# A hybrid of two state-space mixers and two feed-forward parts: the order of the steps behind a chunk's output projection

## The chip, the cores and the metric

The kernel runs on one core of one Trainium2 chip. The metric is the device time of one execution in microseconds (us); the figures of before are the median of three runs, and one further execution was taken by the hardware profiler.

## The reference, cut to what matters

The input is x of 4 sequences, 1024 tokens and 512 features, in float32. Four parts follow one another, each on the layer norm of what stands and added to it: mixer A, a feed-forward part, mixer B, the same feed-forward part again. Both mixers are state-space layers of 1024 inner channels. A has 16 heads of 64 channels and a state of 64, B has 64 heads of 16 channels and a state of 128. What the change touches is this much of a mixer:

```python
gate, hBC, dt = split(x @ in_proj)            # B: the same with factors on the parts
hBC = silu(causal_conv4(hBC) + conv_b)        # h, B, C
dt = softplus(dt + dt_bias)
# per head, over the tokens: state = state * exp(dt * A) + (dt * h) B^T ;  y = C state + D h
yf = y * silu(gate)                           # B: norm first, then the gate
var = mean(yf * yf)                           # over the 1024 channels
out = (norm_w * yf * rsqrt(var + eps)) @ out_proj
```

The kernel works in chunks of 128 tokens: what a chunk's tokens give each other comes from a 128 x 128 matrix of decays for every head, and what earlier chunks give comes from the state carried between chunks.

## The kernel before

**Tiles and stages.** A chunk is 128 tokens, a group is two chunks, and a mixer has 16 groups, so 32 chunks, four groups to a sequence. Two generators are woven together for each group: `chunk`, which runs the state-space part of the present group's two chunks, and `front`, which projects, convolves and gates the group after it. `front` also carries `norm`, the layer norm of the group after that. All four compute engines take their instructions in the order in which Python issues them; only the DMA queue on SyncE is ordered by the scheduler. What waits at the head of an engine's list holds all that stands behind it.

**The weave.** Each `yield` of `chunk` adds an amount to `due`, and steps of `front` are issued until their amounts have used it up. When `front` has nothing left the inner loop ends. Single small matmuls stand in the list `small`: one is issued behind each large matmul of `front` (line 347), and `finish` issues what is left of a part. `later_on` holds instructions for other engines that are issued one step later.

**front.** 18 steps: 8 half gates (product `pz`, line 347; tanh on ScalarE, line 536; `z` on VectorE, line 541) and 9 or 10 convolution tiles (product `pc`, line 347; first tap on ScalarE, line 470; three taps on VectorE, line 474). The small products `pd` for dt (line 503) go between those of gates 0 and 1, and line 511 adds the bias to each on VectorE as soon as it is issued. `softplus` starts at step 6 (lines 548 and 549) and goes on through lines 555 to 601.

**chunk.** In this order, the two mixers alike at the start:

- `fold`, two additions on VectorE that bring the chunk before's squares down to 256 columns (lines 971 and 972);
- `decays(0)`, four products `seg` in four PSUM banks (lines 789 and 799), with exponentials on ScalarE (line 806);
- the first step of the chunk before's `tail`;
- `from_state`: the two products `po` with the state (line 847), weighed on VectorE into `yo` (line 851);
- `hdr` and the state's decay on GpSimd (lines 919 and 928);
- the weighing of the decays on VectorE (line 813), the inner products `py` (lines 860 and 829), the sums into `h` (line 878), the squares (line 881 or 885), the gating on GpSimd (line 882), the state's update (`pst`, lines 898 to 909).

Mixer B goes through `decays` four times (0 to 3), mixer A once.

**tail.** In its first step it issues the 8 matmul pairs of the output projection `pout` (line 670) with the 4 short ones of the squares' sum `ssq` (line 672) between the last of them, and leaves the copy of `pout` (line 679), the scaling of `ssq` (line 680) and the power -1/2 on GpSimd (line 223) for `later_on`. In its second step the factor is finished and x updated (lines 685 and 686), the result stored (line 687, on ScalarE's queue) and its statistics taken (lines 229 to 232). Before, the first step stands behind `decays(0)` and the second behind `decays(1)` in B, and behind the weighing in A.

**prologue.** Thirteen small steps that prepare a chunk: five into the bank `misc` (lines 734 to 750) and eight transposes `tph` of h (line 709), weighed on VectorE into `hdt` (line 713); line 727 scales h by D on ScalarE.

**PSUM.** All products but `py` share one pool `mm` of seven banks; `py` has one bank. A tile of the pool takes a bank when it is first asked for, and its first matmul waits for the last reader of the tile that stood there before.

Of the kernel before, what the change touches and what calls it, by code (L numbers as in the profile page):

```python
# [21 lines left out]
KE = E // P  # L22
# [50 lines left out]
def hybrid_kernel(  # L73
# [37 lines left out]
    nc = tc.nc  # L111
# [38 lines left out]
    ones = const.tile([P, P], F32, tag="ones", name="ones")  # L150
# [96 lines left out]
    def mixer(m, in_w, conv_w, conv_b, dt_bias, A_log, Dv, norm_w, out_w, src, dst, first, stats, last_steps={}):  # L247
# [18 lines left out]
        with stack:  # L266
# [176 lines left out]
            def front(f, behind):  # L443
# [51 lines left out]


                v = sm.tile([P, GC, NH], F32, tag="v", name=f"v_{tag}", bufs=1)
                pds = []

                def project_dt(c, k):  # L500
                    if k == 0:
                        pds.append(mm(f"pd_{tag}_{c}"))
                    nc.tensor.matmul(
                        pds[c][:, :NH],
                        xnT[:, k, HIST + c * P : HIST + (c + 1) * P],
                        w_in[:, k, m.dt0 : m.dt0 + NH],
                        start=(k == 0),
                        stop=(k == KD - 1),
                    )
                    if k == KD - 1:  # L510
                        nc.vector.tensor_add(v[:, c, :], pds[c][:, :NH], dtb)

                defer(v, [lambda c=c, k=k: project_dt(c, k) for c in range(GC) for k in range(KD)], True)

# [29 lines left out]
                def softplus():  # L544

                    finish(v)
                    dt = f.dt = sm.tile([P, GC, NH], F32, tag="dt", name=f"dt_{tag}")
                    nc.vector.tensor_scalar_max(dt, v, 0.0)
                    nc.vector.scalar_tensor_tensor(v, dt, -2.0, v, ALU.mult, ALU.add)
                    yield  # L550
                    exu = wk.tile([P, 512], F32, tag="t2k", name=f"exu_{tag}", bufs=4)
                    ex, u1 = (
                        exu[:, i * GC * NH : (i + 1) * GC * NH].rearrange("p (c h) -> p c h", c=GC) for i in (0, 1)
                    )
                    nc.scalar.activation(ex, v, AF.Exp)
                    yield

                    nc.vector.tensor_scalar_add(u1, ex, 2.0)
                    nc.vector.reciprocal(u1, u1)
                    nc.vector.tensor_mul(ex, ex, u1)  # L560
                    nc.vector.tensor_mul(u1, ex, ex)
                    nc.vector.tensor_scalar_mul(v, u1, LOG_TERMS[0])
                    yield
                    for term in LOG_TERMS[1:-1]:
                        nc.vector.scalar_tensor_tensor(v, v, term, u1, ALU.add, ALU.mult)
                    nc.vector.scalar_tensor_tensor(v, v, LOG_TERMS[-1], ex, ALU.add, ALU.mult)
                    nc.vector.tensor_add(dt, dt, v)
                    yield
                    a = f.a = sm.tile([P, GC, NH], F32, tag="a", name=f"a_{tag}")
                    nc.vector.tensor_mul(a, dt, Ab.unsqueeze(1).to_broadcast([P, GC, NH]))  # L570
                    nc.vector.tensor_scalar(a, a, A_MIN * A_SCALE, 1.0 / A_SCALE, ALU.max, ALU.mult)

                    parts = wk.tile([P, 512], F32, tag="t2k", name=f"parts_{tag}", bufs=4)
                    parts = parts[:, : GC * 2 * HP].rearrange("p (c i h) -> p c i h", c=GC, i=2)
                    if HP > NH:
                        nc.gpsimd.memset(parts, 0.0)
                    hi, lo = parts[:, :, 0, :NH], parts[:, :, 1, :NH]
                    nc.vector.tensor_scalar(hi, a, A_ROUND, A_ROUND, ALU.add, ALU.subtract)
                    nc.vector.tensor_sub(lo, a, hi)
                    yield  # L580
                    yield
                    pcs = mm(f"pcs_{tag}")
                    for c in range(GC):
                        nc.tensor.matmul(
                            pcs[: 2 * HP, c * P : (c + 1) * P],
                            parts[:, c, :, :].rearrange("p i h -> p (i h)"),
                            le,
                            start=True,
                            stop=True,
                        )  # L590

                    rows = slice(0, 2 * HP)
                    ncs = wk.tile([P, 512], F32, tag="t2k", name=f"ncs_{tag}", bufs=4)
                    two = wk.tile([P, 2, GT], F16, tag="two", name=f"two_{tag}")
                    nc.scalar.activation(ncs[rows, :GT], pcs[rows, :GT], AF.Identity, scale=sign[rows])
                    nc.scalar.activation(two[rows, 0], pcs[rows, :GT], AF.Identity, scale=sign[rows])
                    nc.vector.tensor_sub(two[rows, 1], ncs[rows, :GT], two[rows, 0])
                    f.cs = dram.tile([GC, 2 * HP // 4, 2, 4, P], F16, tag="cs", name=f"csd_{tag}")
                    for c in range(GC):
                        for j in range(2):  # L600
                            nc.sync.dma_start(f.cs[c, :, j], two[rows, j, c * P : (c + 1) * P])
                    yield
# [56 lines left out]
            def tail(f, c, sqs):  # L659

                i = f.b * NCH + f.g * GC + c
                tag = f"{m.name}_{i}"
                cols = slice(c * P, (c + 1) * P)


                pout = mm(f"pout_{tag}")
                ssq = mm(f"ssq_{tag}")
                for e in range(KE):
                    on = dict(start=(e == 0), stop=(e == KE - 1))
                    nc.tensor.matmul(pout, f.hs[e // 2][:, e % 2, cols], w_out[:, e, :], **on)  # L670
                    if e >= KE - 2:
                        nc.tensor.matmul(
                            ssq[:, 0:1], sqs[0][:, e - KE + 2, :], ones[:, 0:1], start=(e == KE - 2), stop=(e == KE - 1)
                        )
                po = wk.tile([P, D], F32, tag="t2k", name=f"out_{tag}", bufs=4)
                rs = sm.tile([P, 1], F32, tag="rs", name=f"rs_{tag}", bufs=1)

                def leave():
                    nc.scalar.copy(po, pout)  # L679
                    nc.vector.tensor_scalar(rs, ssq[:, 0:1], 1.0 / E, m.eps, ALU.mult, ALU.add)  # L680
                    rsqrt(rs)

                later_on.append(leave)
                yield
                nc.vector.tensor_scalar_mul(rs, rs, gc)  # L685
                nc.vector.scalar_tensor_tensor(f.xs[c], po, rs, f.xs[c], ALU.mult, ALU.add)
                later_on.append(lambda: nc.scalar.dma_start(dst[i], f.xs[c]))

                layer_stats(sm, f.xs[c], 1e-5, "g", f"g{tag}", out=stats[:, i, 0:2])
                later_on.append(  # L690
                    lambda: nc.vector.scalar_tensor_tensor(
                        stats[:, i, 2:3], stats[:, i, 0:1], -1.0, stats[:, i, 1:2], ALU.mult, ALU.mult
                    )
                )
                yield
# [67 lines left out]
            def chunk(f, c, following):  # L763
# [147 lines left out]

                state.pop("fold", lambda: None)()
                L0 = decays(0)
                next(last, None)
                if not begin:
                    from_state()
                if not end:
                    hdr = wk.tile([P, E], F32, tag="hdr", name=f"hdr_{tag}")
                    nc.gpsimd.tensor_mul(
                        hdr.rearrange("p (n u d) -> p n u d", u=HC, d=HD),  # L920
                        packed(hdt, slice(0, NH // HC)),
                        er.rearrange("p (n u) -> p n u", u=HC).unsqueeze(3).to_broadcast([P, NH // HC, HC, HD]),
                    )
                    if begin:
                        Sp = wk.tile([P, SW], F32, tag="S", name=f"S_{tag}")
                    else:
                        Sp = state["S"]
                        nc.gpsimd.tensor_mul(heads_of(Sp), heads_of(Sp), over_head(et, P, NH // SH))
                yield 2.0
                weigh(L0)  # L930
                if CG == 4:
# [4 lines left out]
                    py, on = open_y(0)  # L936
                    for half in range(2):
                        inner(0, L0, half, py, on)
                    L2 = decays(2)
                    yield 3.0  # L940
                    weigh(L2)
# [15 lines left out]
                else:  # L957
                    next(last, None)
                    yield 2.5
                    to_state()  # L960
                    yield 2.0
                    for half in range(2):
                        py, on = open_y(half)
# [17 lines left out]
            with tc.manual_schedule(  # L981
# [23 lines left out]
                for n in range(len(groups)):  # L1005
# [5 lines left out]
                    for c in range(GC):  # L1011
                        following = (f, c + 1) if c + 1 < GC else (None if ahead is None else (ahead, 0))
                        for us in chunk(f, c, following):
                            due += us
                            while due > 0.0:
                                waiting, later_on[:] = later_on[:], []
                                piece = next(pieces, None)
                                for step in waiting:
                                    step()
                                if piece is None:  # L1020
                                    break
                                due -= piece
                            catch_up()
# [443 lines left out]
```

## Time and profile before

| | |
|---|---|
| median of 3 runs | 3053.41 us (3053.19 to 3053.58) |
| the profiled execution | 3044.65 us, of which its span 3042.9 us |
| granted TensorE clock, mean | 0.963 |
| busy: TensorE, VectorE, ScalarE, GpSimd | 91%, 68%, 41%, 24% |

By stage, from the view of windows:

| stage, us of the span | TensorE busy | VectorE busy | granted clock |
|---|---|---|---|
| first group of A, 0 to 94 | 71.55 | 54.24 | 0.91 |
| mixer A, 94 to 1160 | 1012.67 | 706.09 | 0.98 |
| feed-forward and the start of B, 1160 to 1427 | 247.84 | 154.77 | 0.97 |
| mixer B, 1427 to 2815 | 1255.13 | 1032.13 | 0.96 |
| feed-forward, 2815 to 3043 | 180.75 | 134.44 | 0.94 |

PE is TensorE's matmuls, PEld its weight loads, DVE is VectorE, ACT ScalarE, POOL GpSimd, SP SyncE. A line of a timeline gives the start in the span, the duration, engine, source line, operation, out<-in, shapes, a count, and in brackets how long the engine had been idle and what ended that. In the view of waits a line gives who waited for whom, then the total in us, the number of times and the longest. Names of tiles are shown without their numbers.

### The profile page before, as it was taken

To read this page: it belongs to the slowest core of one execution; us is meant where nothing else is said; L and a number is where in the kernel's file an instruction comes from. 1 tells how busy PE (TensorE), PEld (TensorE's weight loads), DVE (VectorE), ACT (ScalarE), POOL (GpSimd) and SP (SyncE) were. 2 spreads that over 40 slices of the span, in tenths; PEclk is the share of its full clock that TensorE was granted. 3 is DMA by queue.
4 is the path that set the end of the run, shared out by engine and by line. 5 is a ranking of instruction groups with operands and counts; after the bars stand their busy time and mean duration, and the time that the engine had idled before them with its cause. 6 is when DMAs were issued, how large, how long until landed. Compare 5 with 4: busy or idle time off the path is not lost. (4 is left out here: it accounts for less than half of the span.)

```text
span 3042.9 us, 46127 instructions
## 1 busy us (share of the span) xinstructions
PE 2767.9 (91%) x17156; PEld 1789.5 (59%) x17156; DVE 2081.7 (68%) x4417; ACT 1261.8 (41%) x2874; POOL 720.3 (24%) x839
## 2 busy tenths in 40 slices
PE   7999999999999988999999899999888888898986
PEld 5666666666666653456666666666555565564332
DVE  5667666766666662477777687776787777875368
ACT  3334433334333332355444444444444444443245
POOL 1222122122212221351111112212222222212057
PEclk8999999999999999999999999999999999998999
DMA  3000000000000015430000000000000000001423
GB/s 117 14 19 16 16 16 17 24 17 17 16 17 22 10 68 205 154 102 10 17 20 20 13 20 18 13 17 21 22 25 21 20 23 20 13 11 72 170 88 110
DMA packets 92959, 124.25 MB, mean 41 GB/s; under 512 B 38728, under 2 KB 42328, under 8 KB 92736
## 3 DMA queue, kind: packets, MB, share of 16 engines
q1 hardware_dynamic: 80960, 98.23, 10.0%
q10 hardware_dynamic: 9792, 16.82, 1.5%
q0 software_dynamic: 1984, 6.26, 0.6%
q8 instruction: 136, 2.23, 0.3%
q14 instruction: 87, 0.71, 0.1%
HBM read 84.54 MB, written 36.72 MB: 40 GB/s over the span
## 5 line engine op out<-in xcount | busy, mean ns | idle before, releaser
L347 PE MATMUL pc_b<-xnT_b,w_in_b 128*128 128x259 f32 x1280 | 355.7, 408 | 25.1 <-DVE S_b L909 21.9
L813 DVE TENSOR_TENSOR L_b<-L_b,Gm_b 128x1024 f32<-128x1024 f32 x256 | 308.7, 1247 | 2.9 <-ACT L_b L806 2.9
L347 PE MATMUL pz_a<-xnT_a,w_in_a 128*128 128x256 f32 x1024 | 296.5, 408 | 2.9 <-ACT Bt_a L756 2.3
L347 PE MATMUL pc_a<-xnT_a,w_in_a 128*128 128x259 f32 x1152 | 299.1, 394 | 0.0
L806 ACT ACTIVATE L_b<-seg_b 128x512 f32<-128x512 f32 x512 | 263.6, 603 | 74.0 <-PE seg_b L799 74.0
L347 PE MATMUL pz_b<-xnT_b,w_in_b 128*128 128x256 f32 x1024 | 291.4, 397 | 2.9 <-ACT xnT_b L436 2.9
L474 DVE SCALAR_TENSOR_TENSOR u_b<-pc_b,cw_b,u_b 128x256 f32<-128x256 f32 x480 | 231.5, 482 | 79.8 <-ACT u_b L470 68.3
L347 PEld LDWEIGHTS pc_b<-xnT_b,w_in_b 128*128 128x128 f32 x1280 | 229.3, 198 | 92.7 <-DVE S_b L909 25.4
L474 DVE SCALAR_TENSOR_TENSOR u_a<-pc_a,cw_a,u_a 128x256 f32<-128x256 f32 x432 | 208.2, 482 | 73.6 <-ACT u_a L470 63.3
L1205 PE MATMUL g_ps<-gw,xnT_f 128*128 128x512 f32 x512 | 246.9, 619 | 9.6 <-DMA gw<-in_L_ffn_gate_w 4.2
L829 PE MATMUL py_b<-L_b,hdt_b 128*32 128x128 f32 x4096 | 165.7, 299 | 97.6 <-DVE L_b L813 96.5
L670 PE MATMUL pout_a<-w_out_a,h_a 128*128 128x512 f32 x512 | 240.2, 613 | 0.0
L670 PE MATMUL pout_b<-w_out_b,h_b 128*128 128x512 f32 x512 | 235.7, 604 | 0.0
L347 PEld LDWEIGHTS pc_a<-xnT_a,w_in_a 128*128 128x128 f32 x1152 | 200.9, 190 | 58.5 <-DVE rs_a L685 11.4
L882 POOL TENSOR_TENSOR h_b<-h_b,z_b 128x256 f32<-128x256 f32 x128 | 90.8, 730 | 509.5 <-ACT sq_b L881 509.5
L347 PEld LDWEIGHTS pz_a<-xnT_a,w_in_a 128*128 128x128 f32 x1024 | 172.3, 195 | 55.0 <-ACT out_a L679 14.4
L347 PEld LDWEIGHTS pz_b<-xnT_b,w_in_b 128*128 128x128 f32 x1024 | 174.5, 194 | 48.8 <-issue 26.0
L829 PEld LDWEIGHTS py_b<-L_b,hdt_b 128*32 128x32 f32 x4096 | 112.6, 117 | 147.7 <-DVE L_b L813 60.5
L1205 PEld LDWEIGHTS g_ps<-gw,xnT_f 128*128 128x128 f32 x512 | 93.2, 196 | 122.1 <-issue 113.5
L881 ACT ACTIVATE sq_b<-h_b 128x256 f32<-128x256 f32 x128 | 47.9, 417 | 262.5 <-DVE h_b L878 262.5
L670 PEld LDWEIGHTS pout_a<-w_out_a,h_a 128*128 128x128 f32 x512 | 93.3, 192 | 100.1 <-issue 96.3
L670 PEld LDWEIGHTS pout_b<-w_out_b,h_b 128*128 128x128 f32 x512 | 92.3, 190 | 99.5 <-issue 95.7
(321 smaller groups left out, 4919.7 us busy)
## 6 DMA issues: line engine op xcount, KB each, us to landing
d<-in_L_ffn_d_w SPq DMA_DIRECT2D x4, 2048.0 KB
x_f<-xa SPq DMA_DIRECT2D x32, 256.0 KB
xb<-x_b ACTq DMA_DIRECT2D x32, 256.0 KB
x_f<-xb SPq DMA_DIRECT2D x32, 256.0 KB
x_a<-in_L_attn_a_x SPq DMA_DIRECT2D x30, 256.0 KB
xa<-x_a ACTq DMA_DIRECT2D x30, 256.0 KB
out<-x_f SPq DMA_DIRECT2D x22, 256.0 KB
xf<-x_f SPq DMA_DIRECT2D x20, 256.0 KB
```

Of the source, the lines that this page charges most:

```text
L347: nc.tensor.matmul(*args, **kw)
L474: nc.vector.scalar_tensor_tensor(u, ps[:, k : k + GT], cw[:, j, k : k + 1], u, ALU.mult, ALU.add)
L670: nc.tensor.matmul(pout, f.hs[e // 2][:, e % 2, cols], w_out[:, e, :], **on)
L806: nc.scalar.activation(L[:, r], sg[r0 + r], AF.Exp)
L813: nc.vector.tensor_mul(Lr, Lr, Gm.unsqueeze(1).to_broadcast([P, 2 * HB, P]))
L829: nc.tensor.matmul(py[cg * CT : (cg + 1) * CT, e % 4, :], hdt[:, h // HC, u : u + HC, :], Ls[half][:, r, hq, :], start=not started[cg], st ...
L881: nc.scalar.activation(sr, yh, AF.Square)
L882: nc.gpsimd.tensor_mul(yh, yh, zs[half * 2 + r][:, :, cols])
L1205: nc.tensor.matmul(ps, xnT[:, k, :], gw[:, k, :], start=(k == 0), stop=(k == KD - 1 and not bias_on_pe))
```

## The change

The addition of dt's bias is no longer issued behind the product; both additions of a group are gathered in `adding` and issued at the start of `softplus`. The tail has three steps: the output projection with the copy of `pout`; the squares' sum, its scaling and the power; the factor and what follows. In `chunk` the state's products now stand ahead of the tail's first step. In B the second step stays behind `decays(1)` and the third stands behind the first eight-head rounds of `inner(0, ...)`; in A the second stays behind the weighing and the third stands behind `to_state`. Last, where `front` has run out, small steps are issued, each for 0.35 of `due`.

```diff
-                pds = []
+                pds, adding = [], []
...
                     if k == KD - 1:
-                        nc.vector.tensor_add(v[:, c, :], pds[c][:, :NH], dtb)
+                        adding.append(lambda: nc.vector.tensor_add(v[:, c, :], pds[c][:, :NH], dtb))
...
                     finish(v)
+                    for add in adding:
+                        add()
...
                 pout = mm(f"pout_{tag}")
-                ssq = mm(f"ssq_{tag}")
                 for e in range(KE):
                     on = dict(start=(e == 0), stop=(e == KE - 1))
                     nc.tensor.matmul(pout, f.hs[e // 2][:, e % 2, cols], w_out[:, e, :], **on)
-                    if e >= KE - 2:
-                        nc.tensor.matmul(
-                            ssq[:, 0:1], sqs[0][:, e - KE + 2, :], ones[:, 0:1], start=(e == KE - 2), stop=(e == KE - 1)
-                        )
                 po = wk.tile([P, D], F32, tag="t2k", name=f"out_{tag}", bufs=4)
                 rs = sm.tile([P, 1], F32, tag="rs", name=f"rs_{tag}", bufs=1)
+                later_on.append(lambda: nc.scalar.copy(po, pout))
+                yield
+                ssq = mm(f"ssq_{tag}")
+                for q in range(2):
+                    nc.tensor.matmul(ssq[:, 0:1], sqs[0][:, q, :], ones[:, 0:1], start=(q == 0), stop=(q == 1))
 
                 def leave():
-                    nc.scalar.copy(po, pout)
                     nc.vector.tensor_scalar(rs, ssq[:, 0:1], 1.0 / E, m.eps, ALU.mult, ALU.add)
                     rsqrt(rs)
...
                 L0 = decays(0)
-                next(last, None)
                 if not begin:
                     from_state()
+                next(last, None)
...
                     for half in range(2):
                         inner(0, L0, half, py, on)
+                    next(last, None)
                     L2 = decays(2)
...
                     to_state()
+                    next(last, None)
                     yield 2.0
...
                                 if piece is None:
+                                    if small:
+                                        small.pop(0)()
+                                        due -= 0.35
+                                        continue
                                     break
```

## The prediction

> **What bounds the kernel now.** I read the page first, then the view of waits, then the timeline of one group in each mixer.
>
> ```profile
> PE 2767.9 (91%) x17156; PEld 1789.5 (59%) x17156; DVE 2081.7 (68%) x4417; ACT 1261.8 (41%) x2874; POOL 720.3 (24%) x839
> ```
>
> TensorE is the bound, but its idle time differs by stage: 53 us of A's 1066 (windows 94 to 1160) and 133 us of B's 1388 (1427 to 2815). The change moves the work behind these waits; the third line, TensorE's wait for weighed decays, is what B mostly waits for.
>
> ```profile
> DVE yo_a L851 <- PE po_a L847: 124.7, 28, 8.6
> DVE yo_b L851 <- PE po_b L847: 122.0, 55, 7.4
> ...
> PE py_b L829 <- DVE L_b L813: 96.5, 71, 5.8
> ...
> DVE v_b L511 <- PE pd_b L503: 87.8, 32, 7.2
> ...
> PE ssq_a L672 <- DVE sq_a L972: 28.8, 14, 2.7
> ```
>
> VectorE's waits (yo, v) cost only if TensorE then waits for VectorE. TensorE's own wait for the folded squares is the clear price: 28.8 us in A (14 of 16 groups) and 4.3 in B. It is in the second chunk of a group of A:
>
> ```profile
> 511.82 0.62 PE L789 MATMUL seg_a<-later,ident 64*64 64x256 bf16 x8
> ...
> 512.70 6.28 PE L670 MATMUL pout_a<-w_out_a,h_a 128*128 128x512 f32 x14
> ...
> 515.19 1.52 DVE L474 SCALAR_TENSOR_TENSOR u_a<-pc_a,cw_a,u_a 128x256 f32<-128x256 f32 x3 [2.26 <-ACT u_a L470]
> ...
> 517.07 2.04 ACT L806 ACTIVATE L_a<-seg_a 128x512 f32<-128x512 f32 x4
> ...
> 521.16 0.35 PE L672 MATMUL ssq_a<-ones,sq_a 128*128 128x1 f32 x2 [2.19 <-DVE sq_a L972]
> ...
> 524.53 3.09 PE L347 MATMUL pz_a<-xnT_a,w_in_a 128*128 128x256 f32 x10
> ```
>
> The projection runs while ScalarE and VectorE are still 4 to 6 us behind with the convolutions of conv products issued before `seg`. B, first chunk of a group:
>
> ```profile
> 2032.91 0.68 DVE L713 TENSOR_TENSOR hdt_b<-tph_b,dt_b 128x512 f32<-128x512 f32 x1
> ...
> 2033.04 0.30 PE L789 MATMUL seg_b<-later,ident 64*64 64x256 bf16 x2 [0.24 <-DVE S_b L909]
> ...
> 2033.65 2.02 PE L347 MATMUL pc_b<-xnT_b,w_in_b 128*128 128x259 f32 x8
> ...
> 2035.52 0.68 DVE L713 TENSOR_TENSOR hdt_b<-tph_b,dt_b 128x512 f32<-128x512 f32 x1
> 2036.12 0.68 DVE L541 SCALAR_TENSOR_TENSOR z_b<-tz_b,pz_b 128x512 f32<-128x512 f32 x1
> ...
> 2041.38 1.08 PE L829 MATMUL py_b<-L_b,hdt_b 128*32 128x128 f32 x16 [2.31 <-DVE L_b L813]
> ```
>
> Here `seg` of the fourth decays just gets its banks as VectorE leaves them, and TensorE later waits 2.31 us for the fourth weighing.
>
> **What the built order adds: banks.** `pd` holds its two banks to step 6 instead of step 1, and `ssq` asks for its bank later, so every later tile of the seven-bank pool lands elsewhere. I read the changed program's placement and asked of the trace when the bank's last reader ended. Three answers decide:
> - A, second chunk: `po`'s second half stands where conv tile 2 stood (last reader the taps, line 474), and `pout` where `seg` 0 stood (exponential, line 806).
> - B, first chunk: `seg` 3's fourth bank had the second `tph` (last reader the second line 713), and `pc` behind it had gates 2 and 3 (reader line 541).
> - B, first chunk: the second conv product stands where `seg` 2's first bank was (its exponential).
>
> **A, second chunk, per group.** Before, from the end of `seg` to the next gate: 16 matmul passes at 0.428 (starts of neighbouring rows) = 6.85, `ssq` 0.48, the wait 2.15, `po` 1.06 = 10.5; this group took 11.83. After: `po`'s second half waits for the taps that end 515.19 + 1.52 = 516.71, which is 4.0 behind 512.70; then 1.0 for it (one half alone), by when the first exponential (517.07 + 0.58) has ended, then 6.85: 11.9. Over the 15 groups the same reading gives ends between 1.2 earlier and 1.0 later, +0.3 on average. `ssq` still costs 0.5 later on: +0.8 x 15 = +12 us. So the 28.8 us go, and about as much comes back one bank earlier. Queued behind `po`'s second half are the whole projection and the next gate, and ScalarE's copy of `pout` waits for them with the layer norm's copies behind it.
>
> **A, first chunk.** The banks are free. The third step's five VectorE instructions (0.15 + 0.75 + 0.70 + 0.18 + 0.15 = 1.9 us, lines 685 to 232) move from ahead of conv 8's taps to behind the state's update, so Gm (500.01) is about 0.6 later, and line 878, for which `py`'s only bank waits already, 0.75 later: 0 to 0.75 x 15; I take +11, since nothing idles in between.
>
> **B, first chunk, per group**, at 2001 to 2048. `ssq` between the last projections saves 0.45 there; behind `seg` 1 it waits 0.4 for z's bank and takes 0.5. Conv 8's product ends at 2020.5 instead of 2019.95, its taps at 2022.7; line 680, the second weighing 2.35: 2025.1; the third step 1.98: 2027.1; then Gm, the ScalarE chain behind it and conv 9's taps as before (3.1): the third weighing starts at 2030.4 instead of 2028.78. From that start VectorE was without a gap to the second line 713 (7.4 us) and to z (8.0): these end at 2037.8 and 2038.4. TensorE, which wanted `seg` 3 at 2032.5 and `pc` at 2033.65, issues `pc` at 2038.45, +4.8; queued behind `seg` 3 are conv 0 and 1 and the inner products. ScalarE had been busy to 2035.2, so the exponentials are 3.2 later, conv 0's taps 3.3; the two bias additions (2 x 0.224) now stand ahead of the fourth weighing: +3.75 at the place where TensorE waited 2.31 already. x 15 = +56 us. Bounds: bank releases alone, with no later weighing, 2.8 x 15 = 42; the full 4.8 x 15 = 72.
>
> **B, second chunk.** Order saves 0.45, `ssq` takes 0.5, taps come earlier and the third step later; TensorE's wait of 3.0 for the last weighing covers it: 0 to 0.5 x 15, I take +3. Without that cover it is 0.9 a group.
>
> **The rest.** The two VectorE waits (v, yo) are gone for certain; what is next late is the gate's z, at the same place, since it waits for products that moved by 0.45. GpSimd's power moves past a memset of 0.20 us: nothing. ScalarE's store of x moves behind lines 595 and 596, SyncE's reload of that buffer waits for it with two stores and the loads of `upto` and `past` behind: 0 to 1 us a group in A (rows issued 541.3 to 549, wanted at 549.1); I take 0. The small steps issued when `front` is empty change the order in one group of each mixer: 2 us of small products (2777.44 to 2779.46) fill waits, and weighing under the projection saves about 2 more in B, about 3 in A: -7 us.
>
> **The clock.** The wait of 2.15 us at 521 was followed by a slow stretch, the same wait at 452 was not:
>
> ```profile
> 452.00:455.60 3.60, 3.60 (x16) 2.21 (x17) 1.17 (x2) 0.58 (x1) 1.02 (x2) 1.00 0.00 0
> 517.40:521.00 3.60, 1.57 (x4) 0.38 (x2) 3.36 (x11) 1.71 (x4) 0.00 (x0) 1.00 0.00 0
> 521.00:524.60 3.60, 3.44 (x11) 1.48 (x11) 0.01 (x1) 0.58 (x1) 0.00 (x0) 0.71 0.00 0
> ```
>
> In 7 of A's 14 groups matmuls behind the wait took up to twice as long for about 3.5 us, 1.7 lost each. Waits of 3 us should be followed by it more often: +12 in A (0 to 24), +7 in B (0 to 24: there half-clock rows already stand at 2041.4, granted 0.51, and the slow part lies in time that VectorE sets).
> The Trainium skill, page "TensorE: Matmul & The Clock Gate", Part 1, has the rule that speaks against such an exchange: an idle window of some 3.4 us, free-running, halves the clock, and as long a busy one restores it. By that rule a wait of 4.8 us always holds a window and one of 2.15 need not (the trace shows fewer conditions: half of the 2.15 us waits were enough); an estimate from its figure is 1.7 us behind each of B's 15 waits, 26 instead of my 7, and 3166 for the whole.
>
> **Sum.** A: 12 + 11 + 12 = 35; B: 56 + 3 + 7 = 66; ends -7: +94 us. The profiled execution took 3044.65 (span 3042.9 and 1.75 around it), so 3138.7; the runs' median is 8.8 above the profiled one, so 3147.
>
> **Rivals.**
> 1. B's new wait only takes the place of the later one: TensorE stood 2.31 us before the fourth weighing anyway, and if VectorE is not late, only 2.8 - 2.3 = 0.5 a group stays. B: 0.5 x 15 + 3 + 7 = 18; total 35 + 18 - 7 = +46: 3099. For it: ScalarE was busy to 2035.2 anyway. Against: the exponentials themselves wait for `seg` 3. 16%.
> 2. The clock falls behind every new wait: A 24 instead of 12, B 24 instead of 7: +123, 3176. 22%.
> 3. Faster: the folded squares' wait goes and nothing takes its place, -28.8 - 4.3, with A's 7 slow stretches behind it, -12: 3008. It decides where conv 2's taps end within 1.0 us of `seg` instead of 4.0, and the second line 713 ahead of `seg` 3; 8%. For it: VectorE loses over 330 us of waits (yo and v), and might run ahead. Against: those taps wait for ScalarE, which waits for line 417, not for yo.
> 4. No net change, the moves cancelling: 2%.
>
> **How the numbers follow.** My forecast has 52% at 3147. From 0.2% (6 us) on a measurement of this kernel can tell a change from none. Faster 0.08, same 0.02, slower 0.90. The range takes in the second rival, the forecast with its bounds (B 42 to 72, A's clock) and most of the first: 3080 to 3185; outside lie the faster case and the ends.
>
> **What would show it.** `ssq_a` <- `sq_a` gone; new waits of TensorE: `po_a` (or its load) for line 474 of about 3 us in A's second chunks, `seg_b`/`pc_b` for lines 713 or 541 of 4 to 5 us in B's first; `yo` waits of under 1 us. A's stage longer by about 30 us, B's by about 60. I am wrong if TensorE's idle time in B falls below 133 us, or if `po_a` starts right behind `seg_a`.

## The result, and the profile after

The changed kernel takes 3166.43 us (median of 4 runs, 3163.82 to 3168.57) against 3053.49 (4 runs, 3053.19 to 3058.24): 1.0366 of the time before, 95% interval 1.0348 to 1.0384. The profiled execution took 3168.57 us with a span of 3166.9 (before 3044.65 and 3042.9), at a mean granted clock of 0.949 (before 0.963).

The busy times of the page first:

```profile
PE 2843.7 (90%) x17156; PEld 1823.1 (58%) x17156; DVE 2083.6 (66%) x4417; ACT 1260.9 (40%) x2874; POOL 735.8 (23%) x839
```

The counts are those of before and VectorE's time is nearly the same, but TensorE's busy time grew by 75.8 us: the same matmuls took longer. The other 48 of the span's 124 us are standing, and the view of waits says where (who waited <- for whom, total us, times, longest):

```profile
PE py_b L830 <- DVE L_b L814: 50.5, 57, 3.1
...
PE seg_b L790 <- DVE hdt_b L714: 32.6, 23, 2.3
PE pc_b L347 <- DVE S_b L910: 30.7, 12, 2.8
PE po_a L848 <- DVE u_a L474: 29.7, 14, 2.2
...
PE pc_b L347 <- ACT L_b L807: 14.9, 21, 0.7
...
PE pout_b L671 <- POOL xnT_b L429: 7.0, 3, 2.4
PE pout_b L671 <- ACT L_b L807: 6.2, 3, 2.4
...
PE seg_a L790 <- DVE v_a L511: 5.8, 10, 1.0
```

(Lines of the new kernel lie one to six further down: 713 is now 714, 806 is 807, 847 is 848; the taps stay 474.) A's wait for the folded squares is gone, and a wait of the same size for the taps stands in its place. B's wait ahead of the weighed decays fell from 96.5 to 50.5, but new ones for the second hdt product, for exponentials, and of `pout` came, and the one for the state's addition (`S_b`) rose from 21.9 to 30.7. TensorE's idle time from the first `seg` to the last `pout` of a mixer, matmuls and weight loads taken together and gaps of over 0.15 us counted, went from 50.9 to 54.0 us in A and from 132.6 to 175.7 in B.

A's second chunk, TensorE's timeline (start, duration, out<-in, count, and in brackets the idle time before it and what ended that):

```profile
537.08 0.30 PE L790 MATMUL seg_a<-later,ident 64*64 64x256 bf16 x2 [0.41 <-DVE v_a L511]
537.31 0.64 PE L800 MATMUL seg_a<-upto,past 21*128 21x512 f16 x4
537.87 1.12 PE L848 MATMUL po_a<-S_a,Cc_a 64*128 64x512 f32 x2
541.19 1.44 PE L848 MATMUL po_a<-S_a,Cc_a 64*128 64x512 f32 x2 [2.19 <-DVE u_a L474]
542.56 8.44 PE L671 MATMUL pout_a<-w_out_a,h_a 128*128 128x512 f32 x16
...
554.74 0.50 PE L678 MATMUL ssq_a<-ones,sq_a 128*128 128x1 f32 x4
```

Three things are to be seen: `seg` stands for the late addition of dt's bias, `po`'s second half stands for the taps, and the projection behind it takes 8.44 us where an undisturbed one takes 7.13. The clock of these stretches (busy us and count of TensorE, weight loads, VectorE, ScalarE, GpSimd; then the granted clock):

```profile
539.60:543.20 3.60, 2.01 (x3) 0.80 (x4) 3.46 (x9) 2.89 (x8) 0.42 (x1) 0.81 0.00 0
543.20:546.80 3.60, 3.60 (x7) 1.44 (x6) 3.43 (x9) 0.24 (x1) 1.03 (x3) 0.72 0.00 0
546.80:550.40 3.60, 3.60 (x9) 1.52 (x8) 2.39 (x11) 0.00 (x0) 0.00 (x0) 1.00 0.00 0
```

And B's first chunk, all engines, the same chunk as in the prediction:

```profile
2125.80 0.68 DVE L714 TENSOR_TENSOR hdt_b<-tph_b,dt_b 128x512 f32<-128x512 f32 x1
...
2126.53 0.42 PE L790 MATMUL seg_b<-later,ident 64*64 64x256 bf16 x2 [2.31 <-DVE hdt_b L714]
...
2127.43 3.82 PE L347 MATMUL pc_b<-xnT_b,w_in_b 128*128 128x259 f32 x8
...
2135.92 0.64 PE L830 MATMUL py_b<-L_b,hdt_b 128*32 128x128 f32 x16 [0.70 <-DVE L_b L814]
```

The fourth bank of `seg` 3 waits for the second hdt product, and behind it the 8 passes of conv 0 take 3.82 us instead of 2.02: the granted clock was 0.50 in the 3.6 us from 2125.6 and 0.55 in the next.

To place the loss, the table gives for each kernel (the profiled execution) how much longer its chunks were than those of before, a chunk being the time from its first `seg` to the next chunk's; "ends" are the next-to-last chunks of the two mixers, where `front` has run out. A's very first chunk is left out: it moved by -0.8 to +6.8 us, by 5.8 in small_only, whose edit does nothing there. Each row is one execution, so a few us of a column can be chance: small_only's edit reaches the ends alone, yet its other columns move by 0.9 to 2.7.

| kernel | A first | A second | B first | B second | ends |
|---|---|---|---|---|---|
| after | +8.4 | +40.7 | +52.9 | +23.1 | -6.2 |
| bias_only | 0.1 | -13.9 | +66.7 | +10.2 | 0.0 |
| hold_only | 0.0 | -14.0 | +49.4 | +17.0 | 0.0 |
| po_only | -0.8 | +41.8 | -0.3 | +3.3 | -3.3 |
| small_only | +0.9 | +2.0 | +2.5 | -2.7 | -4.0 |
| ssq_only | +11.8 | -46.5 | +6.6 | +0.8 | -4.0 |
| all_but_bias | +8.0 | +43.5 | +16.2 | +21.1 | -6.3 |
| all_but_po | +10.1 | -35.6 | +52.5 | +1.8 | -5.8 |
| ssq_small | +10.6 | -46.5 | +12.8 | +5.3 | -6.1 |
| ssq_early | +1.7 | -44.5 | +8.2 | +5.2 | -5.8 |
| fill_po | +6.7 | +13.7 | +58.8 | +18.7 | -7.4 |

### The profile page after: what moved, and what is told of

It is laid out like the page before. It is cut to its first block, busy times and chain, and to the rows that moved or that the text cites. A ratio compares the mean times of both kernels' runs of the same rounds, so it can differ in the third digit from the quotient of the medians.

```text
span 3166.9 us, 46090 instructions
## 1 busy us (share of the span) xinstructions
PE 2843.7 (90%) x17156; PEld 1823.1 (58%) x17156; DVE 2083.6 (66%) x4417; ACT 1260.9 (40%) x2874; POOL 735.8 (23%) x839
## 5 line engine op out<-in xcount | busy, mean ns | idle before, releaser
L347 PE MATMUL pc_b<-xnT_b,w_in_b 128*128 128x259 f32 x1280 | 388.7, 437 | 48.0 <-DVE S_b L910 30.7
L347 PEld LDWEIGHTS pc_b<-xnT_b,w_in_b 128*128 128x128 f32 x1280 | 248.9, 214 | 118.9 <-DVE S_b L910 34.2
L814 DVE TENSOR_TENSOR L_b<-L_b,Gm_b 128x1024 f32<-128x1024 f32 x256 | 301.3, 1219 | 2.2 <-ACT L_b L807 2.2
L671 PE MATMUL pout_a<-w_out_a,h_a 128*128 128x512 f32 x512 | 253.2, 652 | 0.0
L671 PE MATMUL pout_b<-w_out_b,h_b 128*128 128x512 f32 x512 | 227.9, 599 | 13.2 <-POOL xnT_b L429 7.0
L541 DVE SCALAR_TENSOR_TENSOR z_a<-tz_a,pz_a 128x512 f32<-128x512 f32 x64 | 43.9, 685 | 295.8 <-ACT tz_a L536 295.8
L541 DVE SCALAR_TENSOR_TENSOR z_b<-tz_b,pz_b 128x512 f32<-128x512 f32 x64 | 43.9, 685 | 250.4 <-ACT tz_b L536 250.4
L830 PE MATMUL py_b<-L_b,hdt_b 128*32 128x128 f32 x4096 | 154.4, 288 | 50.8 <-DVE L_b L814 50.5
L671 PEld LDWEIGHTS pout_a<-w_out_a,h_a 128*128 128x128 f32 x512 | 104.5, 210 | 152.5 <-issue 149.9
```

The costliest lines, as they stand in the source:

```text
L347: nc.tensor.matmul(*args, **kw)
L541: nc.vector.scalar_tensor_tensor(z.rearrange("p e t -> p (e t)"), tz, 1.0, pz, ALU.add, ALU.mult)
L814: nc.vector.tensor_mul(Lr, Lr, Gm.unsqueeze(1).to_broadcast([P, 2 * HB, P]))
L830: nc.tensor.matmul(py[cg * CT : (cg + 1) * CT, e % 4, :], hdt[:, h // HC, u : u + HC, :], Ls[half][:, r, hq, :], start=not started[cg], st ...
```

## The experiments

The theory is that the loss comes from the seven banks: which late reader stands in the bank that TensorE asks for next. The main rival is the order, above all the norm's third step that makes VectorE late; a third is the clock. First each part by itself on the kernel before.

**bias_only: the bias additions alone.** The diff's lines with `adding`, nothing else.

> Only the bias additions are moved behind `finish(v)`; all else as before. Theory (banks): pd's two banks held to step 6 push `seg` 3's fourth bank of B's first chunk onto the second `tph` (second hdt weighing) and conv 0's `pc` onto gates 2 and 3 (z), exactly as in the kernel after, so most of B's first-chunk loss comes from this part alone: +2.8 to 3.75 x 15 = +42 to +56; in A's second chunk `seg` takes pd's first bank and waits for the addition, +0.5 to 0.8 x 14 = +7 to +11; in all +50 to +65, 3103 to 3118. TensorE shows waits of `seg_b`/`pc_b` for the hdt and z lines of about 20 to 30 us each. Rival (order): it is the norm's third step that makes VectorE late; moving two additions of 0.22 us costs under 0.5 x 15 = 7: 3053 to 3060, no such waits.

Measured 3111.12 us, ratio 1.0175 (1.016 to 1.019). The waits:

```profile
PE seg_b L791 <- DVE hdt_b L715: 31.5, 19, 2.3
...
PE ssq_a L674 <- DVE sq_a L974: 17.2, 14, 1.2
...
PE pc_b L347 <- ACT L_b L808: 15.1, 21, 0.7
```

This one edit brings B's first-chunk loss whole (+66.7, above the 42 to 56 expected), with the waits of the kernel after and without a third step. The size for A was wrong too: A gained 14 us, and the total came inside its range because the two misses cancel. `seg` does wait for pd's bank, but that splits one wait of 2.2 us into waits of 0.4 to 1.0 and of 1.2, and behind those no projection was slow (the last section).

**po_only: the state's products alone.**

```diff
-                next(last, None)
                 if not begin:
                     from_state()
+                next(last, None)
```

> Only the state's products stand ahead of the output projection; all else as before. Theory (banks): in A's second chunk `po`'s second half takes conv tile 2's bank and waits for its taps, 2 to 3 us in 14 groups, as in the kernel after; the squares' wait at the end of the projection goes since 2 us more lie ahead of it, `pout` behind the wait runs at a low clock: A +1 to +2 a group, +14 to +28; B's placement of `seg` 3 and conv 0 is that of before: 0 to +8. 3067 to 3090. Rival (order alone, the wait for a bank being cheap): the squares' 28.8 us go and nothing comes: 3020 to 3030.

Measured 3093.07, ratio 1.0114 (1.0097 to 1.0131), a little above the theory's range and far from the rival's.

```profile
PE po_a L847 <- DVE u_a L474: 40.9, 14, 3.6
```

The squares' 28.8 us went and 40.9 came, and in 13 of the 14 groups the projection behind the wait took 8.6 to 10.0 us instead of 7.36: +41.8 in A's second chunks alone.

**ssq_only: the tail's three steps alone.** The diff's part of `tail` and the two `next(last, None)` behind `inner(0, ...)` and `to_state()`.

> Only the tail is split into three steps, the squares' sum a step later, the norm's factor as a third step; `po` stays behind `pout`, the bias additions where they were. Theory (banks): in A's second chunk conv tile 2's bank goes to `po`'s first half, which comes 6.85 us behind `seg` when the taps (4.0 behind) are done: the squares' 28.8 us and the slow stretches behind them (about 14 us) go and no wait takes their place: -30 to -42; A's first chunk +11 from the later third step; B's placement of `seg` 3 and conv 0 as before, 0 to +10: 3015 to 3045, faster. Rival (order): the third step behind the eight-head rounds makes B's third weighing 1.6 later and with it all of the first chunk, +1.6 to 3.75 x 15 = +24 to +56, which with A's +11 eats the gain: 3050 to 3080.

Measured 3029.51, ratio 0.9904 (0.9884 to 0.9924): 1.0% faster. A's second chunk:

```profile
503.82 7.13 PE L669 MATMUL pout_a<-w_out_a,h_a 128*128 128x512 f32 x16
510.89 1.13 PE L846 MATMUL po_a<-S_a,Cc_a 64*128 64x512 f32 x4
...
515.95 0.50 PE L676 MATMUL ssq_a<-ones,sq_a 128*128 128x1 f32 x4
```

With the projection first, the taps and the exponentials end beneath its 7.13 us and nothing waits. A's first chunks lose 11.8 us, as predicted for the third step, B's first only 6.6: the rival's price is not there.

**small_only: the small steps at the end of `front` alone.**

> Only the last part: small steps issued where `front` has run out. Both theories: only the last group of each mixer changes, about 3 us less in each: -4 to -8, 3045 to 3050. Rival: the small products go in front of work that was waiting for nothing: 0.

Measured 3050.72, ratio 0.9982 (0.9968 to 0.9995), -5.5 us; in the table the ends give -4.0.

The parts sum to 54.9 + 36.9 - 26.7 - 5.5 = +59.6 us; the whole is +113. The missing 53 are no part's own. The table shows most of it: `po` ahead takes away what the split of the tail gives (-46.5 in A's second chunks alone, but +43.5 beside `po`). By columns the whole is 57 above the parts' sum in A's second chunks and 11 above it in B's second, and 23 below it in B's first.

**hold_only: the bank held, nothing moved.** The kernel before, with the bias added at once, and at step 6:

```diff
+                    for c in range(GC):
+                        nc.vector.tensor_copy(dt[:, c, :1], pds[c][:, :1])
```

> As before, the bias added at once; but at step 6 VectorE reads one column of each of pd's two banks into dt (overwritten by the next instruction), so the banks are held as long as with the bias additions moved, and every later tile lands where it does in bias_only (+55 measured there). Theory (banks): the same cost, since nothing but the hold is left: +50 to +62, 3106 to 3118, with the same waits of seg_b and pc_b for hdt and z. Rival (order: the cost of bias_only came from the two additions standing ahead of the fourth weighing): two reads of about 0.1 to 0.2 us instead, under 5 us: 3056 to 3061.

Measured 3115.80, ratio 1.0194 (1.0167 to 1.0221).

```profile
PE seg_b L791 <- DVE hdt_b L715: 31.4, 20, 2.3
...
PE pc_b L347 <- ACT L_b L808: 15.1, 21, 0.7
```

Two reads of one column, 0.15 us each and of no use but to keep two banks taken, cost as much as the moved additions, with the same waits to 0.1 us. That settles bias_only: the cost is the held banks.

**all_but_bias: the kernel after, bias added at once.**

> The kernel after with the bias additions back behind their products. Theory (banks): B's first chunk goes back to the placement of before, so its +53 goes to 0 to +10; A keeps po's wait (+29 in its second chunks, up to 9 more since `seg` no longer stands for pd's bank ahead of it) and the third step in its first (+11): 3056 + 40 + 5 - 6 = 3095, 3088 to 3106. Rival (order: the third step behind the eight-head rounds makes VectorE late and carries B's first chunk): B keeps most of +53, 3140 to 3150.

Measured 3127.54, ratio 1.0237 (1.0221 to 1.0252), between the two. B's first chunks go back from +52.9 to +16.2, as the theory says though above its 0 to +10, but its second chunks keep +21.1, which neither theory had. There `pout`, now behind `po`, asks for the bank of `seg` 0 before its exponential has run:

```profile
2412.41 1.10 PE L846 MATMUL po_b<-S_b,Cc_b 128*128 128x512 f32 x2 [0.32 <-DVE u_b L474]
2415.89 8.80 PE L669 MATMUL pout_b<-w_out_b,h_b 128*128 128x512 f32 x16 [2.39 <-ACT L_b L805]
```

From a chunk's first `seg` to the second decays this takes 12.1 to 16.3 us in six later groups (before 11.8 to 15.5, ssq_only 11.4), and the last stretch of these chunks grows by 0.8 to 2.0. In ssq_only the first stretch repaid the last; with `po` ahead it doesn't.

**all_but_po: the kernel after, `po` behind `pout`.**

> The kernel after with the state's products back behind the output projection. Theory (banks): A's second chunk loses po's wait and with it the slow projection, keeps the saving of the squares' wait and has `seg`'s wait for pd's bank: -46 + 10; A's first +8; B's first chunk keeps the placement that bias_only and the kernel after share: +50 to +67; B's second falls from +23 to 0 to +5, since `pout` no longer asks for `seg` 0's bank; ends -6: 3055 + 16 to 38 = 3071 to 3093. Rival (the loss is that of the later squares' sum and third step): 3140 or more, as little as 20 under the kernel after.

Measured 3077.43, ratio 1.0078 (1.0061 to 1.0095). Moving `po` back is worth 89 us of the 113: A's second chunks go from +40.7 to -35.6 and B's second from +23.1 to +1.8; B's first keep the cost of the held banks.

**fill_po: work in the wait.** The kernel after, with the first state product of A's second chunks issued three times into its bank:

```diff
-                        nc.tensor.matmul(po, Cc[rows, cols], state["S"][rows, hsl], start=True, stop=True)
+                        for _ in range(3 if CG != 4 and c == 1 and half == 0 else 1):
+                            nc.tensor.matmul(po, Cc[rows, cols], state["S"][rows, hsl], start=True, stop=True)
```

> The kernel after, but in A's second chunks the state's first product is issued three times into the same bank (the same values again), so that TensorE works through the wait for the taps instead of standing: 2 x 1.06 us of more work in waits of 2.0 to 3.1. Theory (clock): behind a TensorE that does not stand the projection runs at full speed, 7.1 instead of 8.3 to 9.5 us: -1.7 x 14 = -24 in A, 3140 to 3146, though there is more work. Rival (the projection is slow for another reason, such as VectorE and ScalarE at work beside it): no change, 3163 to 3170.

Measured 3141.89, ratio 1.0287 (1.0265 to 1.0309), 24.5 us less than the kernel after, with more work. The same group:

```profile
526.45 2.84 PE L849 MATMUL po_a<-S_a,Cc_a 64*128 64x512 f32 x6
529.79 1.09 PE L849 MATMUL po_a<-S_a,Cc_a 64*128 64x512 f32 x2 [0.49 <-DVE u_a L474]
530.81 7.13 PE L671 MATMUL pout_a<-w_out_a,h_a 128*128 128x512 f32 x16
```

The wait for the taps is 0.49 instead of 2.19 and the projection behind it 7.13 instead of 8.44; it was 7.13 in 12 of the 14 groups. VectorE and ScalarE have the same work beside it, so in these groups the slowness had come with the stand. The other two (the chunks from 168.07 and 945.75) show that a stand is not the only thing that it comes with:

```profile
168.99 0.30 PE L790 MATMUL seg_a<-later,ident 64*64 64x256 bf16 x2 [0.41 <-DVE v_a L511]
...
169.77 5.38 PE L849 MATMUL po_a<-S_a,Cc_a 64*128 64x512 f32 x8
175.08 8.88 PE L671 MATMUL pout_a<-w_out_a,h_a 128*128 128x512 f32 x16
```

From the chunk's first `seg` to the projection no row is behind a stand of over 0.41 us (0.97 in the other one), the same as in groups that stayed fast, yet the granted clock was 0.64 from 170.8 and 0.50 from 174.4, for 3.6 us each. Why it fell there stays open.

**ssq_small: the two parts that gain, together.**

> The two parts that gained, together: the tail in three steps and the small steps at the end of `front`; the order of `po` and the bias additions as before. If they add: 3056 - 27 - 5.5 = 3024 (3017 to 3030). If the small steps only filled what the split frees: 3029.

Measured 3025.92, ratio 0.9904 (0.9876 to 0.9932). The runs (3018.09 to 3034.01) do not tell 3024 from 3029.

**ssq_early: the same, A's third step where the second was.**

```diff
-                yield 2.0
+                if CG == 4:
+                    yield 2.0
+                else:
+                    yield 1.0
+                    next(last, None)
+                    yield 1.0
                 weigh(L0)
...
-                    to_state()
-                    next(last, None)
+                    to_state()
```

> ssq_small with one difference in A: the weave's 2.0 ahead of the weighing are cut in two, the squares' sum is issued between them, and the third step stands where the second stood before (behind the weighing), not behind the state's update. Theory (the 10 us that A's first chunks lost in ssq_only and ssq_small come from the third step's VectorE work behind the state's update): they come back, 3026 - 8 to - 10 = 3017, 3011 to 3024, if the folded squares are ready when the sum comes 9 us behind `seg` (they were 8.4 behind it before). Rival: the sum waits for them again, up to 1 us x 14 and a slow stretch here and there: 3026 to 3045.

Measured 3018.64, ratio 0.9887 (0.987 to 0.9903): 1.1% faster than before and 4.7% than the kernel after. The interval overlaps that of ssq_small, so the times alone do not part the two; the table does: A's first chunks come back from +10.6 to +1.7. So their loss came from the third step behind the state's update, as far as one edit shows that moves the squares' sum too. This is the version to keep.

## Why the prediction was right, and where its steps were not

It said 3147, slower; 3166.43 came. The sum was +94, against +113 by the medians' ratio. That it came so near is in part luck: A's and B's second chunks were 17 and 20 too low, and B's first chunk was too high.

- **A, second chunk.** The place was right to the bank: the squares' wait gone, `po`'s second half 2.0 to 2.2 us behind for line 474 in 14 groups. The size was not: 12 for the place and 12 for the clock were forecast, 40.7 came. From the end of `seg` to the gate the 14 groups took 11.4 us on average before and 13.6 after, 29.5 in all. The stands in that stretch are nearly equal (28.8 before, 29.7 after). Without its stand and with no row slow a group takes 8.63 before (10.81 - 2.18) and 9.04 after (12.78 - 2.04 - 1.70), 6 us in 14 groups. What is left is slow rows: 10.6 before and some 33 after, 23.7 of these in the projections (above 7.13 each) and the rest mostly in `po`'s second half, whose passes start up to 0.99 us apart instead of 0.5. So the clock's term was mis-sized: about 23 more where 12 was forecast, and fill_po, which takes away most of it, brings the column down by 27. The other step that failed lies ahead: the reading of banks did not ask what stands for pd's own bank. `seg`'s fourth bank does, and from its first pass to its last `seg` takes 1.6 to 2.3 us instead of 0.95 in 11 groups, 10.9 in all.
- **A, first chunk.** +11 forecast, +10.9 with the first chunk of all (+8.4 without it), and ssq_early shows that the moved third step is the cause.
- **B, first chunk.** +56 and a clock of +7 forecast, +52.9 measured. The banks named were right, and in the chunk worked through, conv 0 started 37.7 us behind the chunk's first `seg` (2127.43 - 2089.7), as the working has it (2038.45 - 2000.7). But the stand there was 2.3 at most, not the 4 to 5 us named as its sign, `pc` stood for line 541 once (0.5), and part of the lateness was there when the fourth decays began, 33.0 us into that chunk instead of 31.6. How the sum was made up was wrong twice. The bank releases alone were put at 42 with the rest from the later third weighing: bias_only, which has no third step, cost 66.7, hold_only 49.4, while the third step without the held banks (ssq_only) cost 6.6. And 3.75 a group was taken for all 15: the first eight cost 3.8 to 6.0, the last seven only 1.0 to 3.0. Six of those seven groups had a wait of 4.1 to 5.8 us for the fourth weighing before (4.10 in chunk 18, against 2.31 in chunk 14) and of 1.1 to 2.3 after: there the new wait mostly took the place of the old one, as the first rival said of all.
- **B, second chunk.** +3 forecast, +23.1 measured: the largest miss. Two steps failed. The first is the cover, TensorE's wait of 3.0 for the last weighing: only chunks 7, 15 and 23 of B (counted from 0) have it, and there it is 3.07 after as before. With the tail split, a conv product stands longer for the state's addition. The line of before, which is 30.7 us in the kernel after:

```profile
PE pc_b L347 <- DVE S_b L909: 21.9, 12, 2.2
```

  Every kernel with the third step has 30.6 or 30.7 here, every one without it 21.9 or 22.0. From the fourth decays on these chunks grew by 15.1, 1.0 a group; the prediction's own price without the cover was 0.9. The second is the order: up to the second decays ssq_only saved 14.4, and the kernel after lost 5.1, since in six later groups `pout` behind `po` stood 1.4 to 2.4 us (for `seg` 0's exponential in three of them by the view). With `po` back behind the projection this stretch saves its 14.4 again and the column falls to +1.8. The placement was read for A's second chunk and not asked for B's.
- **Ends.** -7 forecast, -6.2 measured; -5.5 by small_only's medians.
- **The clock in B**, +7: no run takes it by itself. A count over the trace, of what neighbouring matmuls without idle time between their rows took beyond the median of the same pair of lines where it was over half as much again, gives 173 us in B before and 191 after, so about +18; the same count gives 23 less for fill_po than for the kernel after in A, where 24.5 were measured. It is a rough count: in B, where fill_po changes nothing, it gives 4 more for fill_po.
- **The rivals.** The replacement rival holds in part in the last seven of B's 15 groups, which lost 1.0 to 3.0 and not its 0.5. The faster rival's condition, conv 2's taps done when they are asked for, is what ssq_only arranges by leaving `po` behind the projection, and that was faster by 27 us. The second rival's total, 3176, lies nearer to the result than the forecast, and in A for its reason: the clock fell behind every one of the 14 new waits and cost about 23 more than before, where it allowed 24. In B the rough count gives 18 of its 24. The estimate from the skill's page, 3166, is nearest by luck: it was worked out for B's waits of 4.8 us, and 2.3 was the longest there. Its reading of the rule was wrong too: with free-running windows of 3.4 us only an idle time of 6.8 is sure to hold a whole one, not 4.8, and one of 2.15 cannot hold any.

## What to carry to other kernels

In a pool of banks, moving a reader or a request moves every tile behind it: build the new order and list, for each tile that TensorE asks for next, the last reader of its bank, in every kind of chunk and not only where the first surprise is. Put the long product first and the short ones behind it when banks are still in use, since 7 us of matmuls hide the readers that 1 us doesn't. Parts of a change are to be measured one by one: here one part gained 27 us, and another took it away again.

## What the runs showed of the hardware

- Whether a projection was slow went in most groups by the length of the stand before it, by matmul rows in A's second chunks: after a stand of 1.2 us in none (14 groups of bias_only, 3 of before), after 1.8 in the one of before that had it, after 2.2 in 3 of 7 before, after 2.0 in 2 of 3 of po_only, after 2.0 to 2.2 in 14 of 14 after, after 2.7 and more in all (3 of before, 11 of po_only). By the weight loads' rows the stands of 2.2 us were 2.97 to 3.01 without one. In two groups of fill_po the clock fell with no stand of 1 us before it. The Trainium skill, page "TensorE: Matmul & The Clock Gate", Part 1, gives an idle window of some 3.4 us; here shorter stands were enough, and the measurement decides. Why 2.2 us was enough in all groups of one kernel and in half of the other's stays open.
- It was not foreseen that useless work can pay: 32 repeated products, two in each group, some 1.7 us of passes, made the kernel 24.5 us faster than the kernel after; in 12 of 14 groups the projection behind them was at full speed. Its granted clock was 1.00 from 524 to 538.4 us of the span, through the group shown.
